# The order of two sets of eight products per unit, in an fp32 attention kernel split into fp32r halves

## The chip, the cores and the metric

The kernel runs on one core of a Trainium2 chip. The metric is the time on the device of one execution, in microseconds (us), as the median of several runs. Lower is better.

## The reference

The layer is a self-attention over the pixels of an image, with a residual. There are four images of 64 x 64 pixels with 256 channels, all in fp32:

```python
q = einsum('bwhc,cd->bwhd', x, Wq) + bq        # 128 channels
k = einsum('bwhc,cd->bwhd', x, Wk) + bk        # 128 channels
v = einsum('bwhc,cd->bwhd', x, Wv) + bv        # 256 channels
pq, pk, pv = (t.reshape(B, -1, N) for t in (q, k, v))      # N = 4096
energy = einsum('bcn,bcm->bnm', pq, pk)        # 4096 x 4096 for each image
attention = softmax(energy, axis=-1)
out = einsum('bcm,bnm->bcn', pv, attention).reshape(B, W, H, C)
return gamma * out + x
```

## The kernel before: a unit, and the products of a unit

The kernel works on each image in groups of 256 columns n (16 groups), and on each group in eight units of four blocks of 128 rows m (`t` = 0 to 7). For each unit TensorE first makes the energies of a unit that lies three ahead (twelve matmuls, tiles `sa` and `sb`); ScalarE and VectorE turn energies into exponentials and split each into parts `h`, `l` and `d`. [...]`h` goes with `vh`, `l` with `vl`, and `d` with `vd`, and the three together stand for the fp32 product. The products accumulate over the eight units of a group in PSUM: those of h and l in the two banks `a0` and `a1` (one for each 128 columns, j = 0 and 1), those of d in both halves of the bank `bb`.

A product is one matmul: a block of 128 x 128 of h, l or d is loaded as weights, and a row block of V streams through. That of vh and vl is 258 wide, its last two columns of ones giving the softmax's sum; the tiles keep 260 floats for it. That of vd is 256 wide.

```python
NB, P = 256, 128
NJ, NG, NU = NB // P, N // NB, NM // 4        # 2, 16, 8
STEPS = NG * NU                               # 128 units an image
LOOK = 3
VC = C + 4                                    # 260
...
pool("pad", 1).tile([P, 16], F32, name="pad")       # three small tiles that only shift addresses
ppool = pool("ppool", 2)
pool("pad2", 1).tile([P, 112], F32, name="pad2")
...
vh = qkv.tile([P, NM, VC], F32R, tag="vh", name="vh")
vl = qkv.tile([P, NM, VC], F32R, tag="vl", name="vl")
vd = qkv.tile([P, NM, C], F32R, tag="vd", name="vd")
...
def attend(b, u):
    g, t = divmod(u, NU)
    if t == 0:
        now["acc"] = [ps_o.tile([P, C + 2], F32, tag=f"a{j}", ...) for j in range(NJ)]
        now["bb"] = ps_o.tile([P, NJ, C], F32, tag="bb", ...)
    h, l, d = units[b, u]
    acc, bb = now["acc"], now["bb"]
    for left, right in ((h, vh), (l, vl), (d, vd)):
        for j in range(NJ):
            out_ = bb[:, j, :] if left is d else acc[j]
            back = left is l and j == NJ - 1 and t in (1, 3)
            for i in reversed(range(4)) if back else range(4):
                m = 2 * t + i // 2 + NI * (i % 2)
                nc.tensor.matmul(
                    out_,
                    left[:, i, j * P : (j + 1) * P],
                    right[:, m, : out_.shape[1]],
                    start=(t == i == 0 and (left is h or left is d and j == 0)),
                    stop=(t == NU - 1 and i == 3 and left is not h),
                    skip_group_check=True,
                )
    if t == NU - 1 and (b, g) != (B - 1, NG - 1):
        o = now["o"] = work.tile([P, NJ, C + 2], F32, tag="o", ...)
        for j in range(NJ):
            nc.scalar.activation(o[:, j, :], acc[j], AF.Identity, scale=1.0 + E)
...
for u in range(STEPS):                        # for each image
    ...
    energy(b, ahead, k)                       # k = 0, 1: twelve matmuls in all
    ...
    halves(b, u + 1)                          # l and d of the next unit
    attend(b, u)
```

In the present order a unit's matmuls are twelve energies, then h's eight (four into a0, four into a1), l's eight in the same way, and d's eight into bb. In units 1 and 3 the last four of l run backwards.

Of the kernel before, what the change touches and what calls it, by code (L numbers as in the profile page):

```python
# [20 lines left out]
def kernel(  # L21
# [36 lines left out]
    nc = tc.nc  # L58
    B, W, H, C = x.shape
    P = 128  # L60
# [4 lines left out]
    NI = NM // 2  # L65
# [108 lines left out]
    NJ = NB // P  # L174
    NG = N // NB
    NU = NM // 4
# [22 lines left out]
    with ExitStack() as fast:  # L199
# [18 lines left out]
# [3 lines that stand above are left out]
# [131 lines left out]
        def halves(b, u):  # L352
# [7 lines left out]
            )  # L360
            units[b, u] = h, l, d

        def attend(b, u):

            g, t = divmod(u, NU)
            if t == 0:
                now["acc"] = [
                    ps_o.tile([P, C + 2], F32, tag=f"a{j}", name=f"a{j}_{b}_{g}")
                    for j in range(NJ)
                ]  # L370
                now["bb"] = ps_o.tile([P, NJ, C], F32, tag="bb", name=f"bb_{b}_{g}")
            h, l, d = units[b, u]
            acc, bb = now["acc"], now["bb"]
            for left, right in ((h, vh), (l, vl), (d, vd)):
                for j in range(NJ):
                    out_ = bb[:, j, :] if left is d else acc[j]


                    back = left is l and j == NJ - 1 and t in (1, 3)
                    for i in reversed(range(4)) if back else range(4):  # L380
                        m = 2 * t + i // 2 + NI * (i % 2)

                        nc.tensor.matmul(  # L383
                            out_,
                            left[:, i, j * P : (j + 1) * P],
                            right[:, m, : out_.shape[1]],
                            start=(t == i == 0 and (left is h or left is d and j == 0)),
                            stop=(t == NU - 1 and i == 3 and left is not h),
                            skip_group_check=True,
                        )  # L390
            if t == NU - 1 and (b, g) != (B - 1, NG - 1):
                o = now["o"] = work.tile([P, NJ, C + 2], F32, tag="o", name=f"o_{b}_{g}")
                for j in range(NJ):
                    nc.scalar.activation(o[:, j, :], acc[j], AF.Identity, scale=1.0 + E)
# [89 lines left out]
        for b in range(B):  # L484
# [24 lines left out]
            for u in range(STEPS):  # L509
                g, t = divmod(u, NU)  # L510
# [33 lines left out]
                for forms in beside:  # L544
                    next(forms)
                attend(b, u)
                if (b, u) == (B - 1, STEPS - 1):
                    finish_last(b, g, loads.pop((b, "x", g)))
# [11 lines left out]
    NJ = NB // P  # L560
    NP = NM // 2
    xg, og = columns(x, NB), columns(out, NB)
    with tc.If(nc.values_load(again[0:1, 0:1]) > 0), ExitStack() as general:
# [8 lines left out]
        for b in range(B):  # L572
# [16 lines left out]
            for g in range(NG):  # L589
                ps = []  # L590
                mx = work.tile([P, 2, NB], F32, tag="mx", name=f"gmx_{b}_{g}")
                for t in range(NP):
                    sp = ps_s.tile([P, 2, NB], F32, tag="s", name=f"gs_{b}_{g}_{t}")
                    for h in range(2):
# [4 lines left out]
                            start=True,  # L599
                            stop=True,  # L600
# [31 lines left out]
                for t, p in enumerate(ps):  # L632
# [8 lines left out]
                    for h in range(2):  # L641
                        for s in range(2):
# [4 lines left out]
                                start=(t == h == 0),  # L647
                                stop=(2 * t + h == NM - 1),
# [43 lines left out]
```

## Time and profile before

| | |
|---|---|
| time, median of 3 runs | 2449.05 us (2447.3 to 2449.57) |
| span of the profiled execution | 2445.0 us |
| TensorE clock granted | 0.999 of full speed |
| instructions | 50042, of them 19988 matmuls and as many weight loads |
| matmuls of h and l into a | 8192 |
| matmuls of d into bb | 4096 |
| matmuls of the energies, sa and sb | 4096 and 2048 |

A page of the profile shows each engine's busy time, the chain of work that ended last, followed back from the end, and groups of instructions by line and tile. Matmuls are pipelined: one begins before the one ahead has ended, so their durations add up to more than the span, and the pace is read from the distance of their starts. The chain gives this distance: each matmul on it counts until the next one begins. PEld is TensorE's loading of weights, which runs beside the matmuls.

### The profile page before, as it was taken

To read this page: it belongs to the slowest core of one execution; us is meant where nothing else is said; L and a number is where in the kernel's file an instruction comes from. 1 tells how busy PE (TensorE), PEld (TensorE's weight loads), DVE (VectorE), ACT (ScalarE), POOL (GpSimd) and SP (SyncE) were. 2 spreads that over 40 slices of the span, in tenths; PEclk is the share of its full clock that TensorE was granted. 3 is DMA by queue.
4 is the path that set the end of the run, shared out by engine and by line. 5 is a ranking of instruction groups with operands and counts; after the bars stand their busy time and mean duration, and the time that the engine had idled before them with its cause. 6 is when DMAs were issued, how large, how long until landed. Compare 5 with 4: busy or idle time off the path is not lost.

```text
span 2445.0 us, 50042 instructions
## 1 busy us (share of the span) xinstructions
PE 2434.4 (100%) x19988; PEld 2403.8 (98%) x19988; DVE 2100.4 (86%) x2318; ACT 1797.5 (74%) x3201; POOL 425.8 (17%) x781
## 2 busy tenths in 40 slices
PE   9999999999999999999999999999999999999998
PEld 8999999999899999999989999999998999999998
DVE  5988888888698888888869888888886988888887
ACT  5777777777677777777667777777766777777775
POOL 4211111111411111111141111111114111111110
PEclk9999999999999999999999999999999999999999
DMA  7766666665776666666477666666647766666663
GB/s 233 225 201 213 203 207 202 203 214 156 232 225 197 210 204 207 209 197 212 145 241 229 202 201 207 205 209 201 205 143 245 230 204 198 210 204 209 207 202 114
DMA packets 137407, 498.92 MB, mean 204 GB/s; under 512 B 15536, under 2 KB 57264, under 8 KB 137168
## 3 DMA queue, kind: packets, MB, share of 16 engines
q0 software_dynamic: 92320, 453.17, 59.8%
q1 hardware_dynamic: 44304, 42.22, 5.5%
q8 instruction: 160, 2.62, 0.4%
q14 instruction: 79, 0.65, 0.1%
q10 hardware_dynamic: 544, 0.26, 0.0%
HBM read 445.25 MB, written 50.33 MB: 203 GB/s over the span
## 4 chain that ended last, share of the span: by engine, by line
PE 99%; DMA 0%; DVE 0%; SPq 0%; issue 0%
PE a L383 40%; PE bb L383 19%; PE sa L330 19%; PE sb L330 10%; PE qk L135 5%; PE v L156 5%; PE xt L122 1%; PE ot L415 1%; DMA x<-in_x_dram 0%; SPq L82 0%; DVE o L452 0%; PE ot L457 0%; DVE x L463 0%; PE zp L449 0%; DVE r L441 0%
## 5 line engine op out<-in xcount | busy, mean ns | idle before, releaser
L334 ACT ACTIVATE x<-sa 128x512 f32<-128x512 f32 x1024 | 614.2, 600 | 507.6 <-PE sa L330 505.4
L344 DVE TENSOR_TENSOR x<-x,y 128x1024 f32<-128x1024 f32 x512 | 627.0, 1225 | 228.2 <-ACT y L334 228.2
L330 PE MATMUL sa<-q,k 128*128 128x256 f32 x4096 | 733.2, 279 | 0.0
L355 DVE TENSOR_TENSOR l<-x,h 128x1024 fp32r<-128x1024 f32 x512 | 624.0, 1219 | 0.0
L358 DVE SCALAR_TENSOR_TENSOR d<-h,x 128x1024 fp32r<-128x1024 f32 x512 | 624.0, 1219 | 0.0
L330 PEld LDWEIGHTS sa<-q,k 128*128 128x128 f32 x4096 | 617.9, 188 | 0.4
L334 ACT ACTIVATE y<-sb 128x512 f32<-128x512 f32 x1024 | 615.1, 601 | 0.0
L383 PE MATMUL a<-vh,h 128*128 128x258 f32 x4096 | 574.3, 282 | 0.0
L383 PE MATMUL a<-vl,l 128*128 128x258 f32 x4096 | 571.9, 282 | 0.0
L330 PE MATMUL sb<-q,k 128*128 128x256 f32 x2048 | 566.2, 276 | 0.0
L383 PE MATMUL bb<-vd,d 128*128 128x256 f32 x4096 | 556.3, 278 | 0.0
L314 POOL DMA_DIRECT2D k<-kf x512 | 279.8, 546 | 1566.6 <-PE sb L330 1541.7
L349 ACT ACTIVATE h<-x 128x1024 fp32r<-128x1024 f32 x512 | 543.9, 1062 | 9.1 <-DVE x L344 8.4
L383 PEld LDWEIGHTS a<-vl,l 128*128 128x128 f32 x4096 | 524.6, 189 | 0.0
L383 PEld LDWEIGHTS a<-vh,h 128*128 128x128 f32 x4096 | 522.7, 189 | 0.0
L383 PEld LDWEIGHTS bb<-vd,d 128*128 128x128 f32 x4096 | 513.7, 188 | 0.0
L330 PEld LDWEIGHTS sb<-q,k 128*128 128x128 f32 x2048 | 384.9, 188 | 0.1
L135 PE MATMUL qk<-wqk_sb,xts 128*128 128x256 f32 x512 | 121.1, 379 | 0.0
L156 PE MATMUL v<-xts,wv_sb 128*128 128x256 f32 x512 | 120.3, 379 | 0.0
L156 PEld LDWEIGHTS v<-xts,wv_sb 128*128 128x128 f32 x512 | 97.3, 190 | 13.2
L135 PEld LDWEIGHTS qk<-wqk_sb,xts 128*128 128x128 f32 x512 | 92.3, 190 | 10.0
L275 POOL DMA_DIRECT2D qd<-qks x128 | 69.4, 550 | 179.5 <-DVE qks L144 170.3
(60 smaller groups left out, 868.6 us busy)
## 6 DMA issues: line engine op xcount, KB each, us to landing
k<-kf POOLq DMA_DIRECT2D x512, 768.0 KB, 4.7
x<-in_x_dram SPq DMA_DIRECT2D x128, 256.0 KB, 3.9
kf<-f POOLq DMA_DIRECT2D x64, 384.0 KB, 3.7
out_dram<-x POOLq DMA_DIRECT2D x63, 256.0 KB, 2.5
qd<-qks POOLq DMA_DIRECT2D x128, 64.0 KB, 2.9
qr<-qd SPq DMA_DIRECT2D x64, 128.0 KB, 3.6
wv_sb<-in_L_conv_Wv_dram POOLq DMA_DIRECT2D x1, 256.0 KB, 6.3
out_dram<-x SPq DMA_DIRECT2D x1, 256.0 KB, 3.5
```

The source lines that it names most:

```text
L122: nc.tensor.transpose(tp[:, k, s, :], self.xs[i][:, s, k * P : (k + 1) * P], ident,)
L135: nc.tensor.matmul(qk[:, s, :], self.xt[i][:, k, s, :], wqk_sb[:, k, :], start=(k == 0), stop=(k == KC - 1),)
L156: nc.tensor.matmul(vp[:, eh, :], wv_sb[:, k, eh * P : (eh + 1) * P], self.xt[i][:, k].rearrange("p s a -> p (s a)"), start=(k == 0), stop= ...
L275: nc.gpsimd.dma_start(qd[b, i // 2 + NG // 2 * s][:, i % 2, :], x[:, s, :C2])
L314: nc.gpsimd.dma_start(t.rearrange("p (i s) f d -> p i s (f d)", s=2), kf[b, u % NU])
L330: nc.tensor.matmul(to[:, i], kt[:, 2 * k + i, f, :], q[:, f], start=first, stop=last)
L334: nc.scalar.activation(to[:, 2 * k : 2 * k + 2, :], sp.rearrange("p i j d -> p i (j d)"), AF.Exp, scale=scale,)
L344: nc.vector.tensor_tensor(x, x, y, ALU.mult)
L349: nc.scalar.activation(h, units[b, u], AF.Identity, scale=UPPER)
L355: nc.vector.tensor_tensor(l, x, h.bitcast(F32), ALU.subtract)
L358: nc.vector.scalar_tensor_tensor(d, h.bitcast(F32), 1.0 + E, x, ALU.mult, ALU.subtract)
L383: nc.tensor.matmul(out_, left[:, i, j * P : (j + 1) * P], right[:, m, : out_.shape[1]], start=(t == i == 0 and (left is h or left is d and ...
```

## The change: an order of its own for each unit

The eight products of h and the eight of l in a unit can be done in any order, because they are only summed. The change gives each of the eight units t of a group an order for h's and one for l's. A digit x of the string stands for the product with j = x // 4 and i = x % 4, so that "01234567" is the plain order. The orders were taken from 500 measured random ones. Those of d stay plain. As the first product into a bank is now not always that of i = 0, the start flag is given to the first one that comes for each bank. The aim is to have TensorE run the same matmuls at a better pace.

```diff
+        ORDERS = (
+            ("13564072", "14325076"),
+            ("41256307", "41763502"),
+            ("26147053", "35601472"),
+            ("41236075", "57104632"),
+            ("10436572", "10726543"),
+            ("57164203", "34250167"),
+            ("35042176", "65341027"),
+            ("35210467", "15347062"),
+        )
+
+        def order(f, b, g, t):
+            return "01234567" if f == 2 else ORDERS[t][f]
+
         def attend(b, u):
...
-            for left, right in ((h, vh), (l, vl), (d, vd)):
-                for j in range(NJ):
+            begun = set()
+            for f, (left, right) in enumerate(((h, vh), (l, vl), (d, vd))):
+                for n, x in enumerate(order(f, b, g, t)):
+                    j, i = divmod(int(x), 4)
                     out_ = bb[:, j, :] if left is d else acc[j]
-                    back = left is l and j == NJ - 1 and t in (1, 3)
-                    for i in reversed(range(4)) if back else range(4):
-                        m = 2 * t + i // 2 + NI * (i % 2)
-                        nc.tensor.matmul(
-                            out_,
-                            left[:, i, j * P : (j + 1) * P],
-                            right[:, m, : out_.shape[1]],
-                            start=(t == i == 0 and (left is h or left is d and j == 0)),
-                            stop=(t == NU - 1 and i == 3 and left is not h),
-                            skip_group_check=True,
-                        )
+                    bank = 2 if left is d else j
+                    m = 2 * t + i // 2 + NI * (i % 2)
+                    nc.tensor.matmul(
+                        out_,
+                        left[:, i, j * P : (j + 1) * P],
+                        right[:, m, : out_.shape[1]],
+                        start=(t == 0 and bank not in begun),
+                        stop=(t == NU - 1 and n >= 6 and left is not h),
+                        skip_group_check=True,
+                    )
+                    begun.add(bank)
```

## The prediction

> **What bounds the kernel now.** I read the page's first part, then its chain, then the chain of waits over one group, then the single tiles. The page's first line of engines and the page's chain say that TensorE has work all the time:
>
> ```profile
> PE 2434.4 (100%) x19988; PEld 2403.8 (98%) x19988; DVE 2100.4 (86%) x2318; ACT 1797.5 (74%) x3201; POOL 425.8 (17%) x781
> PE 99%; DMA 0%; DVE 0%; SPq 0%; issue 0%
> ```
>
> The reader is to see that nothing but TensorE's own pace is on the path (99%), and that its weight loads (PEld) are nearly as busy as its matmuls (PE). So a change to the matmuls' order passes into the time one to one, as long as no operand comes late. "Busy" says nothing of the pace; for that I take the chain's time of the matmuls of each line. The chain of waits from 1000.5 to 1005.5 us covers the fourth unit of a group (t = 3); times are start and duration in us:
>
> ```profile
> 1000.70 0.23 PE sa L330 x2
> 1000.93 0.11 PE sb L330
> 1001.04 1.91 PE a L383 x16
> 1002.95 0.92 PE bb L383 x8
> 1003.87 0.23 PE sa L330 x2
> 1004.10 0.11 PE sb L330
> ...
> 1004.78 0.11 PE sb L330
> 1004.89 0.23 PE sa L330 x2
> 1005.12 0.11 PE sb L330
> 1005.23 0.36 PE a L383 x3
> ```
>
> One unit is 5.23 - 1.04 = 4.19 us of back-to-back matmuls: sixteen products of h and l into the two banks of a (1.91 us, 119 ns each), eight of d into bb (0.92 us, 115 ns), and twelve energies (5.23 - 3.87 = 1.36 us, 113 ns each). All of them load 128 weights and stream 256 columns, a's 258. So the ones whose order changes are the slow ones. The tile views say the same of single instructions (minimum/median/maximum in ns):
>
> ```profile
> L383 PE MATMUL a<-vh,h x4096: 276/283/366, 74.7 to 2433.4; 128*128 128x258 f32 x196
> L383 PE MATMUL a<-vl,l x4096: 276/282/288, 75.7 to 2434.4; 128*128 128x258 f32 x196
> L383 PE MATMUL bb<-vd,d x4096: 276/276/287, 76.6 to 2435.3; 128*128 128x256 f32 x196
> ```
>
> A matmul at the full pace lasts 276 ns here, of which most overlaps with the next. bb's median is at this floor; a's median is 6 to 7 ns above it, but a's minimum reaches it. So the same instruction, same shape, is sometimes slow and sometimes not.
>
> **Is the slowness a matter of place in the order?** I compared the same unit in different groups by the chain of waits from 983 to 1020 us; these are t = 1 and t = 2 of one group, and its t = 7:
>
> ```profile
> 992.16 1.91 PE a L383 x16
> 994.07 0.94 PE bb L383 x8
> ...
> 996.86 1.90 PE a L383 x16
> 998.77 0.91 PE bb L383 x8
> ...
> 1017.82 1.93 PE a L383 x16
> 1019.75 0.35 PE bb L383 x3
> ```
>
> In the next group (34.0 us later) the same places show 1.91 + 0.94, 1.91 + 0.92 and 1.93 + 0.92 us, and in the one after it 1.91 + 0.94, 1.90 + 0.91 and again 1.93 us for a. The eight units of a group take, for a plus bb, 2.84, 2.85, 2.81, 2.83, 2.84, 2.84, 2.84 and 2.85 us, and again so in each group. The spread is small and it repeats. What repeats from group to group is the order and the addresses: which row of V streams (t sets it) after which, and which weights load beside it. What differs is the buffer of h (three in turn over eight units), and it makes no difference. So the excess is decided by the sequence of addresses, not by other engines. I chose to believe this; it is what the whole change rests on.
>
> [...]with nothing to wait for, like matmuls lie between 276 and 288 ns. The rows of vh and vl are 260 floats apart, those of vd 256; only a's products slow down, and the first few of bb behind them. I read this as the streams of rows and of weights being in each other's way inside PE's reads[...].
>
> **The change part by part.** It removes and adds no instruction: 24 products a unit before and after, with the same rows, weights, shapes and banks. Only h's eight and l's eight are permuted, differently for each t; d's eight stay. (1) The old rule, which ran l's second four backwards in t = 1 and 3, goes. (2) Products into a0 and a1 now alternate within a run. The energies already alternate between sa and sb, and run at 113 ns, so I give a change of bank no cost. (3) The start flag goes with the first product into each bank; [...]. (4) a1 is needed by the third product of a new group instead of the fifth. The copies of a0 and a1 to o end at 1020.63 us where the next group's first product starts at 1021.87, so 1.2 us are left, more than the 0.24 us by which the need moves forward (timeline). (5) h and l are made a whole unit ahead of their products, so their order meets no new wait.
>
> **The most it could bring.** By the chain of the whole run a's share is 40.0% and bb's 19.3% of 2445.0 us: 978 us over 8192 and 472 us over 4096 products, 119.4 and 115.2 ns each. At the energies' 113.4 ns (sb: 9.5% of 2445.0 over 2048), [...]a's would be 114.2. The excess is 5.2 x 8192 = 42.6 us for a and 1.8 x 4096 = 7.4 us for bb, 50 us in all or 98 ns a unit. Were all of it gone, the time would be 2399 us, 2.04% less. So 2% is just about the end of what can be had.
>
> **What it should bring.** The orders are the best of 500 that were measured. What the best of 500 gives over the mean is about 3 standard deviations, if the times are spread like a bell. I take the spread from the eight units, which differ in rows and so are eight samples of such a sequence: 2.81 to 2.85 us, a standard deviation of about 12 ns by the rounded values (some of it rounding; 8 ns is as likely). Three of these are 24 to 36 ns a unit, over 512 units 12 to 18 us. This supposes that a random order is on average as good as the present one, which I can't read anywhere; the present one has a touch of search in it (the two reversals), which would take a little off. I take 29 ns a unit, 15 us: 2449 - 15 = 2434 us. It leaves 69 of the 98 ns of excess standing.
>
> **The rivals.** *The excess is structural.* a's rows are 1040 bytes apart instead of 1024, and if each costs a fixed extra read, then a product takes about 120 ns in any order and the fluctuation only shifts time from one to the next. For it: the eight units, each with other rows, differ by only 1.4%. Against: a's minimum of 276 ns. It would make the gain 3 to 6 us: 2443 to 2446. *The spread of random orders is larger than that of the eight sorted ones*, since mixing j and i tries pairs that the sorted order never has. Nothing in the profile shows such pairs. If the spread were 20 ns, the gain would be 60 ns a unit, 31 us: 2418. *A bank change, or the later engines, take it back.* DVE is 86% busy and its work is 14% shorter than PE's; a unit of 4.15 us still holds it. Alternating banks may cost after all where products accumulate: 8 more changes of bank a unit at 2 ns each are 8 us: 2457. The energies' 113 ns speaks against this, and measured orders would have shown it.
>
> **Range and chances.** The middle of the sum is 2434; the structural rival sets the upper end, 2446, and the wide spread the lower one, 2417. Faster by over 2% needs the whole excess gone, 1 in 100. Slower by over 2% needs 96 ns more a unit, nearly twice the present excess, 1 in 100. The rest, 98 in 100, lies within 2%, nearly all of it on the faster side.
>
> **What would show it.** In the profile after: PE still 99% of the chain; a's share lower with bb's and the energies' pace unchanged (a's sixteen in 1.88 to 1.89 us, near 117.5 ns each, bb's eight about 0.92); a's median duration nearer to 280 than to 283 ns; the same time for the same t in each group. The prediction is wrong if a's sixteen still take 1.91 us on average (the structural rival), if they fall below 1.86 (the wide spread), if a wait on ACT shows before the first product of a group, or if the energies change their pace although nothing of them changed.

## The result, and the profile after

The changed kernel takes 2436.87 us (2436.62 to 2436.98, 4 runs) where the kernel before takes 2448.18 us beside it (2447.29 to 2449.57). The ratio is 0.9953, with a 95% interval of 0.9936 to 0.9970. That is 11 us less, inside the predicted range of 2417 to 2446 us and 3 us over the predicted 2434. A later pair of measurements gave 2438.72 against 2449.76 us and the same ratio, 0.9953 (0.9937 to 0.9970).

The first part of the profile's page and its chain, after:

```profile
PE 2424.4 (100%) x19988; PEld 2393.4 (98%) x19988; DVE 2099.7 (86%) x2318; ACT 1795.6 (74%) x3201; POOL 424.4 (17%) x781
PE 99%; DMA 0%; DVE 0%; SPq 0%; issue 0%
```

TensorE is busy for 10 us less (2434.4 to 2424.4), the span is 10 us shorter (2445.0 to 2435.2), and the chain is TensorE's as before. What the order gave went straight into the time. The chain of waits from 983 to 1019 us, after, shows the units t = 1, 2 and 3 of one group (start, duration in us):

```profile
988.46 1.90 PE a L398 x16
990.35 0.93 PE bb L398 x8
991.28 0.44 PE ot L431 x4
...
993.13 1.91 PE a L398 x16
995.04 0.91 PE bb L398 x8
...
997.32 1.89 PE a L398 x16
999.20 0.91 PE bb L398 x8
...
1001.47 1.90 PE a L398 x16
```

The lines `ot` are the four transposes of a finished group, which stand between t = 1 and t = 2. t = 3 went from 1.91 + 0.92 to 1.89 + 0.91 us, t = 1 from 1.91 + 0.94 to 1.90 + 0.93, and t = 2, already the shortest, became a little longer in this group (1.90 + 0.91 to 1.91 + 0.91). The twelve energies behind t = 3 are unchanged: 1001.47 - 999.20 - 0.91 = 1.36 us, as before. The tile view, after (minimum/median/maximum in ns), agrees:

```profile
L398 PE MATMUL a<-vh,h x4096: 275/281/365, 75.0 to 2423.3; 128*128 128x258 f32 x196
L398 PE MATMUL a<-vl,l x4096: 275/282/288, 75.9 to 2424.2; 128*128 128x258 f32 x196
L398 PE MATMUL bb<-vd,d x4096: 275/276/286, 76.9 to 2425.1; 128*128 128x256 f32 x196
```

Only h's median fell, by 2 ns. Matmuls overlap: the median product of h lasts 281 ns, and the next matmul starts 119 ns behind its start. So, to see more, I added the distances between the starts of all matmuls in the trace. By these, h's products take 4.5 us less over the run (491.0 to 486.5), l's 3.0 (488.6 to 485.6) and bb's, whose order is the same, 2.7 (473.7 to 471.0); the energies take 707.7 and 708.0 us. So a quarter of the gain lies in bb, behind the products that were reordered: in the units measured below, the first four of bb's eight go from 117.1 to 115.7 ns on average, while the last four take 113.3 before and 113.5 after.

In what follows, "a unit" with a time over 4 us is the distance from its first product of h to the next unit's first product of h, 36 matmuls, for the 436 of 512 units that have nothing else in between. Before, a unit takes 4195 ns on average and its a plus bb 2835 ns; after, 4175 and 2815 ns. The medians of the places t = 0 to 7 are 4193, 4200, 4186, 4187, 4200, 4200, 4193 and 4207 ns before and 4187, 4173, 4168, 4153, 4173, 4187, 4167 and 4180 after. At t = 2 the median hides two times: even groups (and group 1) went from 4187 to 4167 ns, the other odd ones, as the one shown, from 4178 to 4185.

### The profile page after: what moved, and what is told of

It is laid out like the page before. It is cut to its first block, busy times and chain, and to the rows that moved or that the text cites. A ratio compares the mean times of both kernels' runs of the same rounds, so it can differ in the third digit from the quotient of the medians.

```text
span 2435.2 us, 50041 instructions
## 1 busy us (share of the span) xinstructions
PE 2424.4 (100%) x19988; PEld 2393.4 (98%) x19988; DVE 2099.7 (86%) x2318; ACT 1795.6 (74%) x3201; POOL 424.4 (17%) x781
## 4 chain that ended last, share of the span: by engine, by line
PE 99%; DMA 0%; DVE 0%; SPq 0%; issue 0%
PE a L398 40%; PE bb L398 19%; PE sa L330 19%; PE sb L330 10%; PE qk L135 5%; PE v L156 5%; PE xt L122 1%; PE ot L431 1%; DMA x<-in_x_dram 0%; SPq L82 0%; DVE o L468 0%; PE ot L473 0%; DVE x L479 0%; PE zp L465 0%; DVE r L457 0%
```

## The experiments

My theory was that the sequence of row and weight addresses sets TensorE's pace, and the chosen orders are the good end of a spread. The rivals were that mixing is good (or bad) in itself, and that 258 columns cost a fixed extra read. Where an experiment has a single time I rely on its trace, since such a time holds up to 4 us that have nothing to do with the question: in the tile views the first product of h starts at 74.7 us before and 75.0 after, but between 75 and 79 us in the experiments.

### A random order in every unit

As the last two products of a group can now fall into one bank, the stop flag goes to the last one of each bank, here and in the two runs with other lists of orders below.

```diff
-            return "01234567" if f == 2 else ORDERS[t][f]
+            if f == 2:
+                return "01234567"
+            xs = list("01234567")
+            Random(f"{b} {g} {t} {f}").shuffle(xs)
+            return "".join(xs)
```

> A random order for h's and for l's eight products in every one of the 512 units, 64 samples for each place t. Theory (the pace is set by the sequence of addresses; the orders kept are the far end of a spread): a plus bb takes on average 2.83 to 2.85 us a unit, like before, with a standard deviation of 8 to 12 ns, and only a few of the 64 samples of a place are as short as the changed kernel's; time 2445 to 2452 us. Rival (any mixing of the two banks is faster than the sorted order): the mean is 2.81 to 2.82 us, as in the changed kernel, time about 2437 us. Rival (mixing costs and the orders kept only win it back): mean over 2.86, time over 2458 us.

Measured: 2460.8 us, before beside it 2447.6. The mean of a plus bb is 2845 ns, 10 ns over the sorted order and at the upper end of what I expected, and the standard deviation within a place is 11 to 19 ns, on average 15, which is more than I expected. The time is over my range, and over the 2458 us of the rival that mixing costs, although the mean stays under the 2.86 us which that rival asked for. The larger surprise is in the energies, which no order touches. The chain of waits from 984 to 1010 us in this run:

```profile
988.80 0.92 PE bb L404 x8
989.72 0.23 PE sa L331 x2
...
991.08 1.93 PE a L404 x16
...
1006.10 0.94 PE bb L404 x8
1007.04 0.23 PE sa L331 x2
...
1008.46 1.55 PE a L404 x13
```

The first unit's energies take 991.08 - 989.72 = 1.36 us, the second's 1008.46 - 1007.04 = 1.42 us: 113 and 118 ns each. This is not noise but two paces, one of which a whole stretch keeps. Of the 436 units, 30% have all twelve energies at 118 ns, and in every one of them the last products of bb before were at 118 ns too. Before the change bb ended at 113 ns in all 436 units, after it in all but one, and the energies followed. A random unit takes 4221 ns on average, 26 ns more than before: 10 from a plus bb, the rest from energies in the 118 ns pace. The pace at which a unit starts does not pass through its random products: behind a unit that ended at 118 ns, 31% end at 118, behind one that ended at 113 ns, 30%.

The best of the random samples of a place (60 to 64 each) were on average as short as the changed kernel's units: 4180, 4166, 4153, 4173, 4180, 4187 and 4186 ns at t = 0 and 2 to 7, 4175 on average, against the changed kernel's medians, 4174 on average. Only t = 6 is clearly longer, by 20 ns.

### Rows 1024 bytes apart, and 256 columns instead of 258: each alone, then both

The first keeps 258 columns but lays the rows of vh and vl 1024 bytes apart (a row's last two columns are then the next row's first two; the softmax's sums are left out). The second keeps 1040 bytes but streams 256 columns (sums left out but for the first product of a group). The third does both. A test of the softmax's sums at the end, which would start a second, general computation, is switched off in all three. The orders stay those of the changed kernel.

```diff
...
-                        right[:, m, : out_.shape[1]],
+                        right[:, m, :] if left is d else right[:, m * C : m * C + C + 2],   # first: flat rows, 256 floats apart
```

```diff
+                    w = C + 2 if t == 0 and bank not in begun and left is h else C
...
-                        out_, ... right[:, m, : out_.shape[1]],
+                        out_[:, :w], ... right[:, m, :w],                                  # second
```

> The changed kernel, with the rows of vh and vl 1024 bytes apart like vd's instead of 1040, and still 258 columns streamed (the last two are then the first of the next row, so the softmax's sums are left out of what is computed). Theory (the addresses of the rows against those of the weights make the excess): a's sixteen products go to 16 x 114.2 = 1.83 us, bb's eight to 0.91, and the time falls by 512 x (1.90 + 0.92 - 2.74) = 40 us or so, to about 2395 us. Rival (258 columns cost a fixed extra read, wherever the row begins): a's sixteen stay at 1.88 to 1.91 us, time within 5 us of the changed kernel's 2437.

> The changed kernel with 256 columns streamed instead of 258 for vh and vl, rows still 1040 bytes apart (the softmax's sums are left out but for the first product of each group). Theory (addresses): a's sixteen keep most of their excess and take 1.86 to 1.90 us; [...]2425 to 2435 us. Rival (width): they fall to bb's pace, 16 x 113.4 = 1.81 us, time about 2390 us.

Measured: 2469.1 and 2450.2 us, before beside them 2447.6. I had missed both times, and so had the rivals: neither is faster than the changed kernel as a whole, with 4241 and 4200 ns a unit against 4175. The tile views of a and bb, of the run with rows 1024 bytes apart:

```profile
L401 PE MATMUL a<-vh,h x4096: 277/283/368, 75.7 to 2455.3; 128*128 128x258 f32 x196
L401 PE MATMUL a<-vl,l x4096: 280/283/294, 76.7 to 2456.2; 128*128 128x258 f32 x196
L401 PE MATMUL bb<-vd,d x4096: 276/279/288, 77.7 to 2457.2; 128*128 128x256 f32 x196
```

and of the run with 256 columns:

```profile
L399 PE MATMUL a<-vl,l x4096: 274/281/287, 79.3 to 2437.5; 128*128 128x256 f32 x196
L399 PE MATMUL bb<-vd,d x4096: 276/281/286, 80.3 to 2438.4; 128*128 128x256 f32 x196
```

With rows 1024 bytes apart, as vd's are, 258 columns stay slow (by starts 121 ns each; the 114.2 ns that I expected was an estimate, not read from any trace). With two columns less, rows 1040 bytes apart stay slow (118 ns each, 1.89 us for sixteen, as I expected of a alone). And bb, untouched in both, is slower than before: its median is 279 and 281 ns instead of 276; in both, 29% of the units have their energies at 118 ns. So neither change was enough alone with these orders. They had been chosen for rows of 1040 bytes and 258 columns; no run fits new ones to either change alone. I took it that both the place of a row and its length must fit, and did both:

> Both at once: 256 columns streamed and rows 1024 bytes apart for vh and vl, so a's products are in all but their data like bb's (the softmax's sums are left out but for the first product of each group). Each alone made nothing faster. Theory (a stream's start and its length must both fit, or each product takes a step of 6.7 ns more): a's sixteen fall to the floor, 16 x 113.4 = 1.81 us, bb's eight to 0.91 us, time 2449 - 512 x (2.84 - 2.72) = about 2390 us. Rival (a's products are slow because of their bank or their accumulation, not their addresses): a's stay at 1.87 us or more, time over 2420 us.

Measured: 2417.6 us, before beside it 2450.7; between what I expected and what the rival did. The chain of waits from 989 to 1019 us shows why:

```profile
1005.99 1.89 PE a L402 x16
1007.87 0.94 PE bb L402 x8
1008.81 0.24 PE sa L333 x2
...
1010.23 1.85 PE a L402 x16
1012.08 0.91 PE bb L402 x8
1012.99 0.23 PE sa L333 x2
...
1014.35 1.81 PE a L402 x16
1016.16 0.91 PE bb L402 x8
```

All products of h, l, d and the energies are now alike, and they run for whole units at one of two paces. In the first unit everything is at 118 ns (1.89/16, 0.94/8), in the last everything at 113 (1.81/16, 0.91/8). Units take 4240 or 4080 ns. The unit between them is the first of a group, where two products still have 258 columns; every such unit ends in the fast pace, whichever stood before it. The slow one nearly always begins behind the transposes: in 28 of the 32 odd-numbered groups (all but group 1 of each image) the units measured from t = 2 on are at 4240 ns, in the even ones at 4080. The one exception is group 0 of the third image, where it begins at t = 4, in a unit of 4315 ns with a wait among its energies. Between such events no unit changes its pace. This shows that the pace is not in the instructions alone: the same instructions, with the same rows of V and with h, l and d in any of their buffers, keep the pace that something earlier left.

### The weights moved by 64 bytes

```diff
-        pool("pad", 1).tile([P, 16], F32, name="pad")
+        pool("pad", 1).tile([P, 32], F32, name="pad")
-        pool("pad2", 1).tile([P, 112], F32, name="pad2")
+        pool("pad2", 1).tile([P, 96], F32, name="pad2")
```

> The changed kernel with h, l and d 64 bytes further on in memory; V, q, k and everything else stay where they are. Theory (rows against weights): d's products, which ran at the floor, now lose it and take 0.93 us or more for eight, the orders no longer fit and a's sixteen take 1.91 us or more; the energies stay at 113 ns; time over 2445 us. Rival (only the rows' own addresses count, or the width): nothing moves, 2437 us.

Measured: 2469.0 us, before beside it 2447.6. The chain of waits from 1000 to 1012 us:

```profile
1002.66 1.92 PE a L398 x16
1004.58 0.94 PE bb L398 x8
...
1007.34 1.94 PE a L398 x16
1009.28 0.96 PE bb L398 x8
1010.24 0.23 PE sa L330 x2
```

bb's eight take 0.94 to 0.96 us, 118 to 120 ns each. The last four matmuls of bb are on average 117 to 121 ns apart in every unit and never at the floor. Only the addresses of the weights (and of the tiles they are made from) moved, the rows of V did not, so the weights' addresses matter too, and not the rows' alone. That it is the place of rows against weights is my reading; no run moves both by the same distance. a's products are back at 119.2 ns from 118.6: the chosen orders no longer fit. My words that the energies stay at 113 ns did not quite hold: 14% of the units have them at 118, the others at 114 to 115.

### Are the orders good in themselves, do they repeat, and do halves add?

Each unit gets the orders of the next one in the list (`ORDERS[(t + 1) % NU]`):

> The changed kernel with each unit's orders taken from the next unit in the list. Theory (orders fit only the rows they were measured with): the gain is gone and the units are like random ones, mean of a plus bb 2.83 to 2.86 us, some of the eight places leaving the energies at 118 ns; 2450 to 2465 us. Rival (the orders are good in themselves): 2437 to 2442 us.

Measured: 2456.4 us, before beside it 2450.7; a unit takes 4209 ns, near the random 4221, and t = 3 leaves its energies in the 118 ns pace every time (4259 ns). Moved by one place, the orders are worth nothing: they fit the rows of their unit. Other moves were not tried.

The best of the 64 random samples at each place:

> For each place t the pair of orders that was shortest among its 64 samples in the run with random orders. Theory (a unit's time is fixed by its orders and repeats whatever stands before it): the units take what they took there, from one unit's first product of h to the next one's 4180, 4173, 4166, 4153, 4173, 4180, 4187 and 4186 ns, 4175 on average like the changed kernel's, so 2435 to 2440 us; then 500 samples found hardly more than 64 do. Rival (part of a short sample was chance or what stood before it): over 2441 us.

Measured: 2443.6 us, before beside it 2450.7. At t = 4 to 7 the units repeat to within a nanosecond: 4173, 4180, 4187, 4187. At t = 2, right behind the transposes, the even groups repeat (4166 or 4167) and nearly all odd ones take 4271, in the 118 ns pace; in those groups t = 3 behind it takes 4181 instead of 4153. The chain of waits from 1000 to 1060 us has t = 3 of an odd group and of the next, even one:

```profile
1001.20 1.91 PE a L399 x16
...
1005.38 1.90 PE a L399 x16
...
1035.09 1.88 PE a L399 x16
...
1039.24 1.90 PE a L399 x16
```

The first takes (1005.38 - 1001.20) 4.18 us, the second (1039.24 - 1035.09) 4.15, with the same orders. So both sides were partly right, and the time, over 2441 us, was the rival's. Here a unit's time is fixed by its orders and by the pace at which it starts: at t = 3, 4153 ns behind the one and 4181 behind the other. A sample taken behind one pace did not hold behind the other.

Only h's new orders, l's as before:

```diff
-            return "01234567" if f == 2 else ORDERS[t][f]
+            if f == 1 and t in (1, 3):
+                return "01237654"
+            return "01234567" if f else ORDERS[t][f]
```

> Half of the change: h's eight in the changed kernel's orders, l's eight as before (with the reversals in t = 1 and 3). Theory (orders of h and of l were found together; what l leaves decides on bb and the energies): h keeps its part, 9 ns a unit, but some of the eight places leave bb and the energies at 118 ns, 70 to 90 ns a unit there; 2442 to 2460 us. Rival (the halves add): 2443 us or a little less, with all energies at 113 ns.

Measured: 2445.5 us, before beside it 2450.1. The places t = 0 to 5 take 4187, 4174, 4168, 4173, 4180 and 4180 ns (medians), as in the changed kernel but for t = 3, which is 20 ns longer, and t = 5, 7 ns shorter. At t = 6 all groups take 4252 instead of 4167: its energies are in the 118 ns pace. At t = 7 it is 4208 instead of 4180. The chain from 1000 to 1020 us has t = 6 on its own:

```profile
1009.36 1.91 PE a L400 x16
1011.27 0.91 PE bb L400 x8
...
1013.53 1.90 PE a L400 x16
1015.43 0.94 PE bb L400 x8
...
1017.79 1.93 PE a L400 x16
```

t = 5 is (1013.53 - 1009.36) 4.17 us, t = 6 (1017.79 - 1013.53) 4.26. So at t = 6 the new order of l is worth most for what it hands on: the 113 ns pace for bb and the energies.

### A version from what was found

If a row's place and length both have to fit, l can have that: only the sums need the two columns of ones. In this version vl has rows 1024 bytes apart and 256 columns. The softmax's sum is then that of h alone, times the mean ratio of x to h; h is x times 1 - 2^-13, written as fp32r, so the output is scaled by 1 - 2^-13. The sum of l itself is left out of the computation.

```diff
+        vlt = vl.rearrange("p m c -> p (m c)")[:, : NM * C].rearrange("p (m c) -> p m c", c=C)
...
-            for f, (left, right) in enumerate(((h, vh), (l, vl), (d, vd))):
+            for f, (left, right) in enumerate(((h, vh), (l, vlt), (d, vd))):
+                    w = C + 2 if left is h else C
...
-                        out_, ... right[:, m, : out_.shape[1]],
+                        out_[:, :w], ... right[:, m, :w],
...
-    nc.gpsimd.tensor_scalar(gam1, gam, 1.0 + E, None, ALU.mult)
+    nc.gpsimd.tensor_scalar(gam1, gam, (1.0 + E) * UPPER, None, ALU.mult)      # UPPER = 1 - 2^-13
```

> A version meant to be kept: vl without its ones, 256 columns with rows 1024 bytes apart; h keeps its 258 columns and the changed kernel's orders, l the plain one. The sum of h alone then stands for the softmax's sum, corrected by the mean ratio of h to x, 1 - 2^-13. Theory (start and length): l's eight and bb's eight go to 113 ns or close, once the stream has settled after h; 25 to 45 ns a unit less than the changed kernel, 2414 to 2424 us. Rival (h's disorder carries through all of l): l's eight stay at 118 ns, 2432 us or more.

Measured: 2444.2 us, before beside it 2450.7, so 20 us over the upper end of what I expected. Three of the eight places end in the 113 ns pace at 4127 to 4140 ns and one at 4154; t = 1, 3, 5 and 6 end in the slow one at 4239 to 4264. The chain of waits from 1000 to 1020 us has t = 3 and t = 4:

```profile
1001.46 1.88 PE a L401 x16
1003.34 0.94 PE bb L401 x8
...
1005.70 1.89 PE a L401 x16
1007.58 0.91 PE bb L401 x8
```

So I supposed that h's orders, chosen for another l, leave the wrong pace there. To see, I gave h random orders again, with l plain:

> The version with the narrow vl, with a random order for h's eight in every unit and l's eight plain. Theory (a stream of fitting 256-column products runs in one of two lasting states, 113 or 118 ns, and what h leaves decides which): each unit's l, bb and energies are at the one or the other; the places where the run before was bad (t = 1, 3, 5, 6) have units in the good state too, one half to two thirds of all; units in the good state take 4.11 to 4.15 us in all, those in the bad one 4.23 to 4.27; mean 4.16 to 4.20 us, time 2435 to 2452 us. Rival (the place, not the order, decides): t = 1, 3, 5 and 6 stay bad in all samples.

Measured: 2438.4 us, before beside it 2450.1. Every place has both kinds, and 72% of all units end in the 113 ns pace, where I expected one half to two thirds. Units in the 113 ns pace take 4114 to 4180 ns, 4147 on average; those in the slow one 4239 to 4284, 4254 on average; none lies between. It is the order, not the place, that decides. I took for each place the shortest order among units that began and ended in the 113 ns pace, with one order for even and one for odd groups at t = 2, which stands behind the transposes:

```diff
+        ORDERS = ("20641753", "50163742", "42706531", "20576431", "17523604", "10645237", "64217305", "65470213")
...
+            if f:
+                return "01234567"
+            return "17035246" if t == 2 and g % 2 else ORDERS[t]
```

> The version with the narrow vl, and for each place the order of h that was shortest in the run before among those that left the good state and came from a unit in the good state (t = 2 has one order for even and one for odd groups). Theory (orders fix a unit's time, the state passes on): from one unit's first product of h to the next one's 4.11 to 4.15 us at each place, 4.13 on average, against 4.175 in the changed kernel; all energies but those after the transposes at 113 ns; 2411 to 2420 us, 0.985 to 0.989 of before. Rival (part of it does not repeat, as in the run with the best of 64): 2425 us or more.

> The changed kernel once more, beside the version with the narrow vl on the same chip: 2435 to 2440 us, 0.994 to 0.997 of before; its trace shows the same eight units' times as the first, 2.79 to 2.83 us for a plus bb.

Measured, on the same chip: 2417.73 us (2414.95 to 2418.13), 0.9865 of before (0.9849 to 0.9882), and for the changed kernel 2438.72 us, 0.9953 (0.9937 to 0.9970), with the same medians of the eight places as in its first trace, to within 1 ns. The page of the new version, and its chain of waits from 984 to 1018 us (t = 2 to 4):

```profile
PE 2405.1 (100%) x19988; PEld 2373.5 (98%) x19988; DVE 2099.8 (87%) x2318; ACT 1798.2 (74%) x3200; POOL 426.0 (18%) x782
```

```profile
987.89 1.86 PE a L403 x16
989.76 0.91 PE bb L403 x8
...
992.03 1.85 PE a L403 x16
993.87 0.91 PE bb L403 x8
...
996.14 1.86 PE a L403 x16
998.00 0.91 PE bb L403 x8
```

The unit takes 4131 ns against 4175 in the changed kernel, as expected, and bb is at the floor nearly everywhere (113.4 on average). The only units of the 436 in the slow pace are t = 2 of group 1 in each image (4255 ns): they have the order for odd groups, whose sample came from group 7, and in the run with both changes, too, the transposes left group 1 and group 7 in different paces. 44 ns times 512 are 22 us; 21 were measured. l's products now take 114.2 ns each, h's still 118.8.

## Why the prediction was right, and where not

- **TensorE's pace passes one to one into the time.** Right: the chain stayed 99% TensorE, and the change took 10 us from its busy time and from the span.
- **The sequence of addresses decides.** Right in the main: orders moved to another unit lose all (4209 ns), moving the weights by 64 bytes takes the floor from bb. But it was incomplete. The pace at which a unit starts counts too, and it passes over products that no order touches. I had seen only that the excess repeats from group to group; that shows it is determined, not by what. Nor does it quite repeat "again so in each group". The prediction's own lines had 1.90 + 0.91 and then 1.91 + 0.92 us for t = 2, which takes 4187 ns in even groups and 4178 in nearly all odd ones. That rows and weights are in each other's way inside TensorE's reads stays a reading. The runs show that the addresses of both count: with the weights moved by 64 bytes bb's eight take 118 to 120 ns each, and 256 columns take 118 ns with rows 1040 bytes apart and 113 or 118 with 1024. They do not show where the two meet.
- **"This supposes that a random order is on average as good as the present one."** Wrong. Random orders are 10 ns worse in a plus bb and 26 ns worse by the whole unit, since 30% of them leave the energies in the 118 ns pace. The sorted order with its two reversals had avoided that in all 436 units.
- **"A standard deviation of about 12 ns", three of them, "24 to 36 ns a unit".** Both terms were mis-sized, and their errors cancel by luck. By exact starts the eight sorted units differ by a standard deviation of 8 ns; random orders within a place differ by 15. And the chosen orders lie two deviations below the random mean, not three: 2845 - 2815 = 30 ns, where I had 29. What stayed uncancelled is the mean: less the 10 ns by which the sorted order is better than random, 20 ns a unit are left, 10.2 us. I had 15 us. Why 500 samples reach no lower than 64 did is not shown. It looks like an edge on the short side, but in the random run a plus bb spreads alike to both sides: 1% lie over 33 ns below their place's mean, 1% over 35 ns above it.
- **"A's sixteen in 1.88 to 1.89 us".** They take 1.90, 118.6 ns each, after 1.91 before. The gain I had put into a is 15 ns a unit there, and 5 ns in bb. l's median stayed at 282 ns.
- **The structural rival.** It was nearer than I gave it credit for: of 98 ns of excess I left 69 standing, and about 78 stand. The 98 are an estimate of mine: they set a's floor at 114.2 ns, over the energies' 113.4, and that two columns more cost this difference was not shown. With 113.4 ns as the floor of all, the chain's shares give 6.0 x 8192 = 49.2 us for a and 56.5 us with bb, an estimate of 110 ns a unit, of which about 90 stand; 2.3% less time would then have been the end, not 2.04%. The rival's mechanism as put, a fixed read for rows 1040 bytes apart, does not fit: 258 columns at 1024 bytes are no faster (121 ns against 118.6), with the orders left as they were. That both together reach 113 ns, in the 113 ns pace, is shown.
- **The wide-spread rival.** The spread was wider (15 ns against 8), but the time did not go where this rival put it: the mean of random orders is worse, and the chosen ones lie only two deviations below it.
- **A bank change costs nothing.** Not settled. Random orders are slower on average (2845 ns against 2835 for a plus bb), and they differ from the sorted one in both banks and addresses; no run separates the two. Nor does one test the start flag alone.
- **The later bank, the waits on ACT, DVE.** None shows: the chain has 0% of DVE and does not list ACT.
- **The energies' pace unchanged.** True for the change (707.7 us before, 708.0 after), and, as the experiments show, an achievement of these orders and not a matter of course.

## What to carry to other kernels

When matmuls that wait for nothing have different spacings, compare the same instruction in two places of the trace: here a stream of alike matmuls keeps 113 or 118 ns for as long as nothing disturbs it, and part of the cost of a disturbance lies in what comes after it (16 of the 26 ns a unit by which random orders are slower). So measure an order by the whole stretch up to the next one, with the stretch before it as it will be, and look first at whether rows, their length and their place against the weights can be made to fit; that, with orders to suit, gave another 21 us where the orders alone gave 11. When a change is "the best of many measured", ask for the mean and the shape of the many, not only for their spread.

## What the hardware showed that I had not expected

- Matmuls of 128 weights and 256 columns run at 113.3 or at 117.8 ns (4080/36 and 4240/36), and the pace lasts over units of 36 matmuls and whole groups, with other engines' work the same.
- Many units' times lie on steps of 6.67 ns, to within 1 ns: 4187, 4193, 4200 and 4207 in the kernel before and 4153, 4167, 4173, 4180 and 4187 in the changed one (medians of places), and 4080 is 612 such steps, 17 for each matmul. 4240 is 636, or 53 for three matmuls. It is no rule: t = 2 takes 4178 in most odd groups before, and with rows 1024 bytes apart there are units of 4203 and 4230 ns.
- Two columns fewer, or rows at "better" addresses, can make a kernel slower than it was, when the orders stay (2450 and 2469 us against the changed kernel's 2437).
- What in TensorE holds the pace, and why the transposes leave the slow one in odd groups (but for group 1) and not in even ones, no run here settles. The transposes read o, which has two buffers in turn, so odd and even groups read other addresses; no run moves them.
